# Late loads, first messages and the order of the head in a graph-convolution kernel

## The chip, the core and the metric

One core of a Trainium2 chip runs the whole program in one launch. The metric is the device time of one execution in microseconds (us); the value for a version is the median of its runs. The core has five instruction streams: PE (TensorE, matrix products), DVE (VectorE), ACT (ScalarE), POOL (GpSimd) and SP (SyncE, used here for DMA issues alone). DMAs are issued by SP, ACT or POOL and carried by 16 DMA engines that all of them share.

## What is computed

The reference is one layer of a graph network over 12500 nodes with 128 features and 400000 edges, which are sorted by `dst`:

```python
h   = maximum(layernorm(x), 0) @ W_in2f.T
Wij = (smu(edge_attr @ W_f1.T + b_f1) @ W_f2.T + b_f2) * edge_weight[:, None]
agg = segment_sum(h[dst] * Wij, src)
out = x + smu(agg @ W_o1.T + b_o1) @ W_o2.T + b_o2
```

In the kernel `dst` is thus the node that an edge reads from (its row of h), and `src` the node that its message is added to.

## The kernel before, in words

The 400000 edges are 3125 tiles of 128. Four tiles are a group (`GRP`), eight a super-group (`SUP`). For each group the kernel makes the filter of its 512 edges, fetches their rows of h, multiplies the two, and sends the products, called messages, to buckets in DRAM (`buf`), one bucket for each block of 128 target nodes. A message is one tile of 128 rows of 129 floats; one indirect DMA on POOL (L572) scatters it, so there are 3125 of these. The edges are cut into nine epochs with a set of buckets each. While the messages of epoch k are sent, the buckets of epoch k-1 are read back and added up by matmuls with one-hot matrices (L617) into `agg`. After the last epoch comes the sum of its buckets and the output layers, with no messages left to send.

Within the main block the order of the instructions of PE, DVE, ACT and SP is the order in which the code writes them (`manual_schedule`); POOL's is left to the scheduler. Each engine works through its stream in order, and waits where an operand is not there yet.

A group g passes through small functions: `bins` (DVE) and `count` (PE) find how many earlier edges went to each bucket; `read` (ACT, four activations with an accumulated result) and `number` (DVE) turn that into row indices; `hide` (PE), `bend` (ACT, Gelu), `smooth` (DVE) and `weigh` (PE) make the filter; `pick` (DVE), `gather` (PE) and `take` (ACT) fetch rows of h from a window of 128 rows; `mix` (DVE) multiplies; `turn` (PE) transposes the product; `send` scales it by the edge weights (ACT, L569), casts the row numbers within the target block (DVE, L566) and issues four messages (POOL, L572). The loop runs these for different groups in one round: `turn(g)` and `send(g)` at its start, then the later parts of g+1, the earlier parts of g+2, `bins(g+3)`. Tiles of `ms` have six buffers, tiles of `ix` eight, `pu`, `pc`, `ph`, `pw` and `pt` in PSUM one each. Between these, `step()` takes pieces of other work (the rest of h, L701 to L719), and SP issues the clearing of the first epoch's buckets (L742 to L746).

`load(s)` prefetches for super-group s: `f` (edge attributes, from the fourth on), `rbc` (the edges' rows relative to the window, read back from `rel_dram` and spread over all partitions) and `hw` (the window, read from `h_dram`). In the loop it runs three super-groups ahead.

Ahead of the loop stands the head, written out by hand:

- L345 to L357: loads of the first 512 columns of indices, the first four blocks of x (`HEAD`), weights, the first weights of edges, and one clearing, issued on SP and ACT.
- L358 to L367: the late loads, ten DMAs issued on ACT: the other 94 blocks of x (three parts of 31 blocks, and the last block of 84 rows), the other columns of `w_sb`, two weights and three biases. A part of x is 31 x 128 rows of 512 bytes.
- L644 to L652: the first chunk of `dst` is made relative to its windows, transposed on PE (L308), copied by ACT (L314) and written to `rel_dram` by SP (L315).
- L653 to L659: statistics of four blocks, their deviations (`deviations`: ACT Sqrt, L184, then a reciprocal on DVE), and their rows of h: normalise, transpose, Relu, product with `w_in`, and a split into three bfloat16 parts (L189 to L215), written to `h_dram` by SP (L214).
- L660: `load` for three super-groups.
- L662 to L683: the first groups' functions, up to `mix(0)` (L677), `smooth(1)`, `bins(1)`, `count(1)`, `read(1)`, `pick(1)`, `bins(2)`. `turn(0)` and `send(0)` come at the loop's start.

Activation functions of ACT live in tables; where another table is needed, an ACT_TABLE_LOAD stands in its stream.

Of the kernel before, what the change touches and what calls it, by code (L numbers as in the profile page):

```python
# [9 lines left out]
F32 = mybir.dt.float32  # L10
# [3 lines left out]
AF = mybir.ActivationFunctionType  # L14
# [5 lines left out]
P = 128  # L20
# [19 lines left out]
def gnn_kernel(  # L40
# [19 lines left out]
    nc = tc.nc  # L60
    N, D = x.shape
    R, E = f_t.shape
    NT = E // P
    assert D == P and E % P == 0
    NB = (N + P - 1) // P
    LASTB = N - (NB - 1) * P
    def chunks(total, step):
        return [(a, min(step, total - a)) for a in range(0, total, step)]

    def bin_rows(t, b, n):  # L70
        return t[b * P:(b + n) * P, :].rearrange("(b p) f -> p b f", p=P)
# [4 lines left out]
    for n in PARTS:  # L76
        n = min(n, left)
# [17 lines left out]
    const = ctx.enter_context(tc.tile_pool(name="const", bufs=1))  # L95
# [10 lines left out]
    eps = const.tile([P, 1], F32, name="eps")  # L106
# [20 lines left out]
    CH = 4 * P  # L127
# [9 lines left out]
    w_sb = const.tile([P, NT], F32, name="w_sb")  # L137
# [7 lines left out]
    b2row = const.tile([1, P], F32, name="b2row")  # L145
    b1 = const.tile([P, 1], F32, name="b1")
    bz = const.tile([P, 1], F32, name="bz")
    w_o1 = const.tile([P, P], F32, name="w_o1")
    w_o2 = const.tile([P, P], F32, name="w_o2")
    bo2 = const.tile([P, P], F32, name="bo2")  # L150
# [5 lines left out]
    def clear(k, c, engine):  # L156

        b, n = cleans[c]
        if b == NB - 1:
            m = CAP[k] * ROW // ZP  # L160
            rows = bufs[k][b * CAP[k]:(b + 1) * CAP[k], :].rearrange("(p s) r -> p (s r)", p=ZP)
            for o, w in chunks(m, zero.shape[1]):
                engine.dma_start(rows[:, o:o + w], zero[:, :w])
            return None
        m = (CAP[k] - ZMIN[k]) * ROW // ZP
        rows = bufs[k][b * CAP[k]:(b + n) * CAP[k], :].rearrange("(b c) r -> b c r", c=CAP[k])[:, ZMIN[k]:, :]
        return engine.dma_start(rows.rearrange("b (p s) r -> p b (s r)", p=ZP),
                                zero[:, :n * m].rearrange("p (b m) -> p b m", b=n))
# [3 lines left out]
    HEAD = 4  # L172
    BY = 44
    x_sb = agg.rearrange("p (b d) -> p b d", d=D)
# [73 lines left out]
    with tc.tile_pool(name="ld", bufs=4) as ld, \  # L248
# [106 lines left out]
            fill(i)  # L355
        nc.vector.memset(zero, 0.0)
        clear(0, len(cleans) - 1, nc.scalar)  # L357
        nc.vector.memset(x_sb[:, NB - 1, :], 0.0)  # L358
        for a, n in chunks(NB - 1 - HEAD, 31):
            nc.scalar.dma_start(x_sb[:, HEAD + a:HEAD + a + n, :], bin_rows(x, HEAD + a, n))  # L360
        nc.scalar.dma_start(x_sb[:LASTB, NB - 1, :], x[(NB - 1) * P:N, :])
        nc.scalar.dma_start(w_sb[:, CH:NT], w_col[:, CH:NT])
        nc.scalar.dma_start(w_o1, w_o1_t)
        nc.scalar.dma_start(w_o2, w_o2_t)
        nc.scalar.dma_start(b1, b_o1.rearrange("o p -> p o"))
        nc.scalar.dma_start(b2row, b_f2)
        nc.scalar.dma_start(bo2, b_o2.to_broadcast([P, P]))  # L367

        groups = [(t0 + a, g) for t0, nt in sups for a, g in chunks(nt, GRP)]
        NG = len(groups)  # L370
# [3 lines left out]
        loaded, onehot, bins_of, slots, hidden, taken = {}, {}, {}, {}, {}, {}  # L374

        def load(s):
            if s >= NS:
                return
            t0, nt = sups[s]
            e0, n = t0 * P, nt * P  # L380
            fb = fbufs[s % NF]
            if s > 2:
                nc.sync.dma_start(fb[0:R, :n], f_t[:, e0:e0 + n])
            rb = ld.tile([P, SUP * P], BF, name="rbc")
            nc.sync.dma_start(rb[:, :n], rel_dram[:, e0:e0 + n].to_broadcast([P, n]))
            hw = ld.tile([P, 3 * D], BF, name="hw")
            at = nc.sync.value_load(base_i[0:1, s:s + 1], min_val=0, max_val=N)
            nc.sync.dma_start(hw, h_dram[bass.ds(at, WIN), :])
            loaded[s] = (fb, rb, hw)

        def pick(s):

# [107 lines left out]
        def smooth(g):  # L500
            if g >= NG:
                return
            n = groups[g][1] * P
            sm = edge.tile([P, GRP * P], F32, name="sm")
            nc.vector.scalar_tensor_tensor(sm[:, :n], units_of.pop(g)[:, :n], LIN, hidden[g][:, :n],  # L505
                                           op0=ALU.mult, op1=ALU.add)
            hidden[g] = sm
# [36 lines left out]
        def mix(g):  # L544
            if g >= NG:
                return
            n = groups[g][1] * P
            mt = edge.tile([P, GRP * P], F32, name="mt")
            nc.vector.scalar_tensor_tensor(mt[:, :n], pws.pop(g)[:, :n], b2, rows_of.pop(g)[:, :n],  # L549
                                           op0=ALU.add, op1=ALU.mult)  # L550
            mixed[g] = mt

        def turn(g):

            n = groups[g][1]
            pt = ps1.tile([P, GRP, P], F32, name="pt")
            mt = mixed.pop(g)
            for j in range(n):
                nc.tensor.transpose(pt[:, j, :], mt[:, j * P:(j + 1) * P], ident)  # L559
            mixed[g] = pt  # L560

        def send(g):

            t, n = groups[g]
            ms = msg.tile([P, GRP, ROW], F32, name="ms")
            nc.vector.tensor_copy(ms[:, :n, P], lo_b[:, t:t + n])  # L566
            pt = mixed.pop(g)
            for j in range(n):
                nc.scalar.activation(ms[:, j, 0:P], pt[:, j], AF.Copy, scale=w_sb[:, t + j:t + j + 1])  # L569
            k, ix = epoch[g // PER], taken.pop(g)  # L570
            for j in range(n):
                i = nc.gpsimd.indirect_dma_start(  # L572
                    out=bufs[k][:, :], out_offset=bass.IndirectOffsetOnAxis(ap=ix[:, j:j + 1], axis=0),
                    in_=ms[:, j, :], in_offset=None)

                apart(i, f"slots{k}", f"slots{k}")
                if g < BY:
                    apart(i, "cleared", "filled")

        def apart(i, others, own):  # L580
            tc.declare_no_dep(i.ins, group=others, reason="slots are disjoint")
            tc.add_to_no_dep_group(own, i.ins)
# [67 lines left out]
        one["lowered"]()  # L650
        one["turned"]()
        one["written"]()  # L652
        nc.vector.tensor_scalar(w_f2, w_f2, GC, None, op0=ALU.mult)  # L653
        for b in range(HEAD):
            stats(edge, b)
# [2 lines left out]
        for step in rows_of_h(0, HEAD, *[rw[:, j * GRP:(j + 1) * GRP, 0:P] for j in range(3)], hs, bank):  # L658
            step()  # L659
        for s in range(3):  # L660
            load(s)
        one["binned"]()  # L662
        bins(0)
        hide(0)
# [10 lines left out]
        number(0)  # L675
        take(0)
        mix(0)  # L677
        smooth(1)
        bins(1)
        count(1)  # L680
# [52 lines left out]
        for g in range(NG):  # L733
            s = g // PER
            k = epoch[s]
            g0, ng = eps_of[k][0] * PER, min(eps_of[k][1] * PER, NG - eps_of[k][0] * PER)
            i = g - g0
            if g % PER == 0:
                load(s + 3)
            if i == 0:  # L740
                cleared = 0
            if g < BY:  # L742

                while at_first < min(len(cleans) - 1, -(-(g + 1) * (len(cleans) - 1) // (BY - 6))):
                    apart(clear(0, at_first, nc.sync), "filled", "cleared")
                    at_first += 1  # L746
            elif k + 1 < EPOCHS:
                past = BY if k == 0 else 0
                upto = min(len(cleans), -(-(i + 1 - past) * len(cleans) // (ng - 4 - past)))
                while cleared < upto:  # L750
                    clear(k + 1, cleared, nc.sync)
                    cleared += 1
            if k and i == 0:
                work = [(b, q) for b in range(NB) for q in range(Q[k - 1])]
                done = 0
            if k and i == 1:
                begin(k - 1)
            if k and i == WAIT - 2:
                choose(k - 1, 0)
            lo = hi = 0  # L760
            if k and i >= WAIT:
                lo = len(work) * (i - WAIT) // (ng - WAIT)
                hi = len(work) * (i + 1 - WAIT) // (ng - WAIT)
            turn(g)
            send(g)
            step()
            number(g + 1)
            weigh(g + 1)
            gather(g + 1)
            take(g + 1)  # L770
            parts(k - 1, lo + (hi - lo) // 2)
            mix(g + 1)
            step()
            hide(g + 2)
            bend(g + 2)
            count(g + 2)
            read(g + 2)
            smooth(g + 2)
            if g % PER == 0:
                pick((g + 4) // PER)  # L780
            bins(g + 3)
            parts(k - 1, hi)
            step()
            assert k == 0 or taken_steps == COUNT and next(h_steps, None) is None
# [51 lines left out]
    with tc.If(flag > 0):  # L836
        with tc.tile_pool(name="gl", bufs=1) as gl, tc.tile_pool(name="gps", bufs=1, space=PSUM) as gps:
# [9 lines left out]
            fb = gl.tile([R + 1, P], F32, name="gfb")  # L847
# [116 lines left out]
```

## Time and profile before

| | us |
|---|---|
| median of three runs | 4244.77 |
| lowest, highest | 4242.52, 4252.45 |
| the profiled execution, whole | 4248.45 |
| its span in the trace | 4246.6 |
| PE busy | 3736.8 (88%) |
| DVE busy | 3220.9 (76%) |
| POOL busy | 3017.8 (71%) |
| ACT busy | 2830.2 (67%) |

The span runs from the first to the last instruction of the profiled execution. "Busy" leaves out register, branch and semaphore instructions and the issuing of DMAs by SP and ACT; the indirect DMAs of POOL are counted[...]. In the views, `ACTq` and `SPq` rows are the DMA issues of ACT and SP, and their length is the issue, not the transfer. Matmuls are pipelined, so a high share of PE is not PE at its peak. The granted clock of TensorE was 0.97 of full speed on average over the span.

### The profile page before, as it was taken

To read this page: it belongs to the slowest core of one execution; us is meant where nothing else is said; L and a number is where in the kernel's file an instruction comes from. 1 tells how busy PE (TensorE), PEld (TensorE's weight loads), DVE (VectorE), ACT (ScalarE), POOL (GpSimd) and SP (SyncE) were. 2 spreads that over 40 slices of the span, in tenths; PEclk is the share of its full clock that TensorE was granted. 3 is DMA by queue.
4 is the path that set the end of the run, shared out by engine and by line. 5 is a ranking of instruction groups with operands and counts; after the bars stand their busy time and mean duration, and the time that the engine had idled before them with its cause. 6 is when DMAs were issued, how large, how long until landed. Compare 5 with 4: busy or idle time off the path is not lost. (4 is left out here: it accounts for less than half of the span.)

```text
span 4246.6 us, 74532 instructions
## 1 busy us (share of the span) xinstructions
PE 3736.8 (88%) x18497; PEld 2320.1 (55%) x18794; DVE 3220.9 (76%) x8578; ACT 2830.2 (67%) x11057; POOL 3017.8 (71%) x3133
## 2 busy tenths in 40 slices
PE   5877788999988999979998979998999799898976
PEld 2334434655555655546555546665666566565755
DVE  5886777877767877768877768887888688787865
ACT  4777777776666767657766757776777576676621
POOL 3777777777777777777777777777777777777620
PEclk9999999999999999989999989999999999999988
DMA  7855665766647666756666657775899699786754
GB/s 216 227 148 162 180 173 179 210 205 193 200 145 217 206 197 204 199 156 202 213 196 199 179 176 205 215 214 167 231 231 235 188 246 233 209 233 177 206 165 122
DMA packets 512380, 834.71 MB, mean 197 GB/s; under 512 B 84576, under 2 KB 323398, under 8 KB 511810
## 3 DMA queue, kind: packets, MB, share of 16 engines
q1 hardware_dynamic: 380986, 601.70, 51.8%
q0 software_dynamic: 100000, 206.60, 15.8%
q10 hardware_dynamic: 30952, 21.54, 1.8%
q8 instruction: 152, 2.49, 0.3%
q14 instruction: 290, 2.38, 0.2%
HBM read 456.16 MB, written 373.36 MB: 195 GB/s over the span
## 5 line engine op out<-in xcount | busy, mean ns | idle before, releaser
L572 POOL DMA_INDIRECT buf<-ms,ix x3125 | 3016.8, 965 | 1051.5 <-issue 249.2
L617 PEld LDWEIGHTS pg<-se,rw 128*128 128x128 f32 x8036 | 1096.5, 193 | 158.6 <-issue 21.2
L569 ACT ACTIVATE ms<-pt,w_sb 128x128 f32<-128x128 f32 x3125 | 905.1, 391 | 342.3 <-DMA buf<-ms,ix 163.6
L617 PE MATMUL pg<-se,rw 128*128 128x128 f32 x8036 | 1118.7, 276 | 10.4 <-DVE se L604 10.4
L467 ACT ACTIVATE jk<-pc,nbig 128x98 f32<-128x98 f32 x3125 | 1027.7, 351 | 6.1 <-PE pc L438 5.4
L539 PE MATMUL pw<-sm,w_f 128*128 128x512 f32 x1564 | 883.5, 647 | 40.6 <-DVE sm L505 35.4
L549 DVE SCALAR_TENSOR_TENSOR mt<-pw,b,hg 128x512 f32<-128x512 f32 x782 | 582.8, 745 | 348.2 <-ACT hg L528 345.9
L497 ACT ACTIVATE ge<-pu 128x512 f32<-128x512 f32 x782 | 468.4, 599 | 558.8 <-PE pu L489 537.0
L489 PE MATMUL pu<-f,w_f 128*128 128x512 f32 x1564 | 812.3, 601 | 4.2 <-DVE sm L505 4.1
L559 PE MATMUL pt<-ident,mt 128*128 128x128 f32 x3125 | 495.3, 281 | 298.8 <-DVE mt L549 295.8
L604 DVE TENSOR_TENSOR se<-irow_ps,rw 128x1536 f32<-128x1536 f32 (+1 forms) x345 | 587.5, 1703 | 145.8 <-DMA rw<-buf 125.2
L505 DVE SCALAR_TENSOR_TENSOR sm<-pu,ge 128x512 f32<-128x512 f32 x782 | 535.0, 684 | 209.7 <-ACT ge L497 200.8
L467 ACT ACTIVATION_READ_ACCUMULATOR jk<-pc,nbig 128x1 f32 x3125 | 674.5, 216 | 0.0
L528 ACT ACTIVATE hg<-ph 128x512 f32<-128x512 f32 x782 | 469.1, 600 | 305.3 <-PE ph L520 303.8
L520 PE MATMUL ph<-oh,hw 128*128 128x512 bf16 (+1 forms) x2049 | 631.8, 387 | 16.1 <-issue 0.4
L559 PEld LDWEIGHTS pt<-ident,mt 128*128 128x128 f32 x3125 | 352.9, 142 | 389.7 <-DVE mt L549 382.5
L424 DVE TENSOR_TENSOR co<-co,po 128x98 f16<-128x98 f16 x2353 | 502.6, 214 | 81.1
L520 PEld LDWEIGHTS <-hw 128*128 128x128 bf16 x2346 | 232.9, 99 | 553.6 <-issue 453.7
L410 DVE TENSOR_TENSOR po<-irow_ps,hi_b 128x392 f16<-128x392 f32 x782 | 433.1, 554 | 0.0
L539 PEld LDWEIGHTS pw<-sm,w_f 128*128 128x128 f32 x1564 | 236.8, 191 | 169.7 <-DVE sm L505 164.7
L489 PEld LDWEIGHTS pu<-f,w_f 128*128 128x128 f32 x1564 | 253.6, 196 | 27.9 <-DVE sm L505 5.6
L437 PE MATMUL pc<-co,ones_h 128*128 128x392 f16 x782 | 258.3, 330 | 3.5 <-DVE co L424 3.5
(104 smaller groups left out, 1702.0 us busy)
## 6 DMA issues: line engine op xcount, KB each, us to landing
rw<-buf SPq DMA_DIRECT2D x292, 774.0 KB
rbc<-rel_dram SPq DMA_DIRECT2D x390, 256.0 KB
buf<-zero SPq DMA_DIRECT2D x243, 387.0 KB
buf<-ms,ix POOLq DMA_INDIRECT x3125
buf<-zero SPq DMA_DIRECT2D x193, 258.0 KB
hw<-h_dram SPq DMA_DIRECT2D x391, 96.0 KB
rw<-buf SPq DMA_DIRECT2D x49, 645.0 KB
f<-in_f_t SPq DMA_DIRECT2D x390, 80.0 KB
```

The lines of the kernel that those rows point to most:

```text
L424: nc.vector.tensor_add(co[:, j], co[:, j - 1], po[:, j - 1])
L467: nc.scalar.activation(jk, pc[:, j], AF.Relu, bias=nbig, accum_out=sl[:, j:j + 1])
L489: nc.tensor.matmul(pu[:, :n], w_f1, loaded[g // PER][0][:, o:o + n], start=True, stop=True)
L505: nc.vector.scalar_tensor_tensor(sm[:, :n], units_of.pop(g)[:, :n], LIN, hidden[g][:, :n], op0=ALU.mult, op1=ALU.add)
L520: nc.tensor.matmul(ph[:, :n], hw[:, q * D:(q + 1) * D], oh[:, o:o + n], start=(q == 0), stop=(q == 2))
L539: nc.tensor.matmul(pw[:, :n], w_f2, hidden.pop(g)[:, :n], start=True, stop=True)
L549: nc.vector.scalar_tensor_tensor(mt[:, :n], pws.pop(g)[:, :n], b2, rows_of.pop(g)[:, :n], op0=ALU.add, op1=ALU.mult)
L559: nc.tensor.transpose(pt[:, j, :], mt[:, j * P:(j + 1) * P], ident)
L569: nc.scalar.activation(ms[:, j, 0:P], pt[:, j], AF.Copy, scale=w_sb[:, t + j:t + j + 1])
L572: i = nc.gpsimd.indirect_dma_start(out=bufs[k][:, :], out_offset=bass.IndirectOffsetOnAxis(ap=ix[:, j:j + 1], axis=0), in_=ms[:, j, :], in ...
L604: nc.vector.tensor_tensor(se[:, :m], irow_ps.unsqueeze(1).to_broadcast([P, m, P]), rows_in[c][:, :m, P:P + 1].to_broadcast([P, m, P]), op= ...
L617: nc.tensor.matmul(pgs[0][:, g, :], rows_in[c][:, o, 0:P], sel[c][:, o, :], start=(q == 0), stop=(q == Q[k] - 1))
```

## The change

The late loads become a function, `late_loads()`, that is called behind the first rows of h; their issuing engine becomes GpSimd. Ahead of each part of x and of the columns of `w_sb`, one column of the destination is set to zero by VectorE, so that these loads wait for that instruction. In the place where the late loads stood, one dummy activation with Sqrt is run. `load(s)` loses its last part, the window of h, which becomes `window(s)`; the first three `load`s come ahead of the first statistics, the three `window`s stay behind the writing of h. `turn(0)` and `send(0)` move from the loop to the place right behind `mix(0)`.

```diff
@@ in place of L358 to L367
-        nc.vector.memset(x_sb[:, NB - 1, :], 0.0)
-        for a, n in chunks(NB - 1 - HEAD, 31):
-            nc.scalar.dma_start(x_sb[:, HEAD + a:HEAD + a + n, :], bin_rows(x, HEAD + a, n))
-        nc.scalar.dma_start(x_sb[:LASTB, NB - 1, :], x[(NB - 1) * P:N, :])
-        nc.scalar.dma_start(w_sb[:, CH:NT], w_col[:, CH:NT])
-        nc.scalar.dma_start(w_o1, w_o1_t)
-        nc.scalar.dma_start(w_o2, w_o2_t)
-        nc.scalar.dma_start(b1, b_o1.rearrange("o p -> p o"))
-        nc.scalar.dma_start(b2row, b_f2)
-        nc.scalar.dma_start(bo2, b_o2.to_broadcast([P, P]))
+        spare = const.tile([P, 1], F32, name="spare")
+        nc.scalar.activation(spare, eps, AF.Sqrt)
+
+        def late_loads():
+
+            nc.vector.memset(x_sb[:, NB - 1, :], 0.0)
+            parts_of_x = chunks(NB - 1 - HEAD, 31)
+            for a, n in parts_of_x:
+                nc.vector.memset(x_sb[:, HEAD + a, 0:1], 0.0)
+            for a, n in parts_of_x:
+                nc.gpsimd.dma_start(x_sb[:, HEAD + a:HEAD + a + n, :], bin_rows(x, HEAD + a, n))
+            nc.gpsimd.dma_start(x_sb[:LASTB, NB - 1, :], x[(NB - 1) * P:N, :])
+            nc.vector.memset(w_sb[:, CH:CH + 1], 0.0)
+            nc.gpsimd.dma_start(w_sb[:, CH:NT], w_col[:, CH:NT])
+            nc.gpsimd.dma_start(w_o1, w_o1_t)
+            nc.gpsimd.dma_start(w_o2, w_o2_t)
+            nc.gpsimd.dma_start(b1, b_o1.rearrange("o p -> p o"))
+            nc.gpsimd.dma_start(b2row, b_f2)
+            nc.gpsimd.dma_start(bo2, b_o2.to_broadcast([P, P]))
@@ load(s)
-            hw = ld.tile([P, 3 * D], BF, name="hw")
-            at = nc.sync.value_load(base_i[0:1, s:s + 1], min_val=0, max_val=N)
-            nc.sync.dma_start(hw, h_dram[bass.ds(at, WIN), :])
-            loaded[s] = (fb, rb, hw)
+            loaded[s] = (fb, rb)
+            if s > 2:
+                window(s)
+
+        def window(s):
+
+            hw = ld.tile([P, 3 * D], BF, name="hw")
+            at = nc.sync.value_load(base_i[0:1, s:s + 1], min_val=0, max_val=N)
+            nc.sync.dma_start(hw, h_dram[bass.ds(at, WIN), :])
+            loaded[s] += (hw,)
@@ the head
         one["written"]()
+        for s in range(3):
+            load(s)
         nc.vector.tensor_scalar(w_f2, w_f2, GC, None, op0=ALU.mult)
...
             step()
         for s in range(3):
-            load(s)
+            window(s)
+        late_loads()
         one["binned"]()
...
         mix(0)
+        turn(0)
+        send(0)
         smooth(1)
@@ the loop
-            turn(g)
-            send(g)
+            if g:
+                turn(g)
+                send(g)
             step()
```

## The prediction

> **What bounds the kernel now.** I read the groups of instructions first, to find the engine that sets the pace. Columns: line, engine, operation, output<-inputs, count | busy us, mean ns | idle us just before it, and what ended most of that.
> ```profile
> L572 POOL DMA_INDIRECT buf<-ms,ix x3125 | 3016.8, 965 | 1051.5 <-issue 249.2
> ```
> GpSimd (POOL) scatters 3125 messages at 0.965 us each; the timeline below shows 0.30 us of issue between neighbours, so 1.27 us a message at best. Then the stretches (length, busy us and count by engine, granted clock, DMA share, GB/s):
> ```profile
> 8.00:36.00 28.00, 3.00 (x6) 1.05 (x6) 2.78 (x14) 4.06 (x6) 0.00 (x0) 1.00 1.01 293
> 59.00:110.00 51.00, 43.66 (x153) 19.69 (x155) 41.82 (x140) 38.73 (x154) 37.05 (x39) 0.96 0.88 224
> 1200.00:1800.00 600.00, 543.59 (x2669) 334.52 (x2707) 452.01 (x1200) 416.77 (x1652) 454.79 (x472) 0.97 0.66 194
> ```
> From 1200 to 1800 there are 472 messages in 600 us, 1.27 us each: exactly POOL's pace, with PE close behind (544 of 600 us). The first message starts at 58.58 and the last ends at 4069.85; 3125 x 1.27 = 3969, so stalls of POOL after its start are only 4011 - 3969 = 42 us. Behind the last message stand 177 us of final sums, which the change leaves alone. So the time is start of the first message + 3969 + 42 + 177, and a change at the head counts nearly in full. What sets the start is in the timeline (start us, length us, engine, line, operation; ACTq and SPq are DMA issues):
> ```profile
> 7.43 0.34 ACTq L163 DMA_DIRECT2D buf<-zero  x1
> ...
> 9.29 6.69 ACTq L360 DMA_DIRECT2D agg<-in_x  x1
> ...
> 16.44 6.33 ACTq L360 DMA_DIRECT2D agg<-in_x  x1
> 22.86 6.89 ACTq L361 DMA_DIRECT2D agg<-in_x  x1
> ...
> 32.68 1.28 ACT L314 ACT_TABLE_LOAD   x1 [16.27 <-DMA agg<-in_x]
> 33.98 0.60 ACT L314 ACTIVATE oh<-pg 128x512 bf16<-128x512 f32 x1
> 34.59 1.28 ACT L184 ACT_TABLE_LOAD   x1
> ...
> 35.88 0.30 ACT L184 ACTIVATE rstd<-mv,eps 128x4 f32<-128x4 f32 x1
> ...
> 43.61 0.41 SPq L214 DMA_DIRECT2D h_dram<-hs  x1
> ...
> 58.58 1.11 POOL L572 DMA_INDIRECT buf<-ms,ix  x1 [57.01 <-ACT ms L569]
> 59.99 0.96 POOL L572 DMA_INDIRECT buf<-ms,ix  x1 [0.30 <-issue]
> ...
> 64.68 0.96 POOL L572 DMA_INDIRECT buf<-ms,ix  x1 [1.20 <-ACT hg L528]
> ```
> ScalarE's queue sits in late loads from 8.0 to 32.65 us, because the transfers fill the 16 DMA engines (share 1.01, 293 GB/s) and the issue waits for room. L314's input, the transposes of L308, had ended at 11.87, L184's (the last statistics) at 12.37. The whole front of the kernel waits in that queue.
>
> **The change, part by part.**
>
> *Late loads off ScalarE.* Ten DMA issues leave. The root's table is asked for by a dummy activation at 7.8, ready near 9.3, while ScalarE would only wait. L314 then starts at 11.9 and ends at 12.5; L184 follows at 12.53 instead of 35.88: **-23.35 us**. That contains one table load of 1.28 (two stood behind the queue, one is left, under cover). Copy needs none of its own: L208 and L212 run as Copy behind L184 with no load between. From rstd to the writing of h is a chain of arithmetic (35.88 to 43.61, 7.7 us), so h goes out near 20.3.
>
> *Targets read back ahead of h.* SP's rbc loads wait for rel_dram's write (then issued near 12.5), which lands long before 20.3, so h is not held back on SP. Behind h, three window loads follow each other without rbc loads between. Taken at nothing: before, hw0 was issued at 46.41 and used at 50.80 with PE busy in between, and the 0.87 us that VectorE waited for rbc is not on PE's chain. If the write were late, h and everything after it would wait on SP; there are some 5 us of cover.
>
> *The memsets.* One 128x128 memset (0.17) moves behind h's last part and four of one column (0.06 each, by eps's row) are new on VectorE, ahead of binned, bins(0) and smooth(0), for which PE waits: 0.17 + 4 x 0.06 = **+0.4 us**. They also hold the x and w_sb loads back until 20.7.
>
> *First messages early.* Before, mix(0) ends at 53.72, but turn(0) stood behind count(1), which waits for bins(1) and began at 55.78; transposes 56.31, ms activations 57.90, message 58.58. Moved, transposes run from 53.75, the activations from about 54.6, the message at about 55.3: **-3.3 us** for message 1. But group 1's first message (64.68) hangs on its own chain, relieved only of turn(0)'s 1.06 us on PE and some of ScalarE: **-0.9 us**. POOL sends four messages in 5.1 us and waits again. What lasts is group 1's shift: -23.35 + 0.4 - 0.9 = **-23.8**, and for message 1 it is -26.2, a start at 32.4.
>
> *Late loads on POOL.* The disputed cost: no plain DMA on POOL is in this trace. POOL is idle from 20.7 to 32.4, so 11.7 us are covered; beyond that each us delays message 1, and all that follow. Each x part has 31 x 128 = 3968 rows of 512 bytes. Ends: if an instruction costs what an indirect one does whatever its rows, ten cost at most 10 x 1.27 = 12.7 us, five of which have no memset to wait for and can go in the idle head: nothing on the path. If the 0.965 us of 128 rows is all per row (7.5 ns), a part costs 29.9 us and three 89.7. In between stands the nearest row for the same transfers: 6.3 to 6.9 us of issue each, when the queue waits for the engines to drain it; the ten took 24.6 us on ScalarE. By that row POOL is held until 20.7 + 24.6 = 45.3 and message 1 starts near 45.6: -13 us.
> The Trainium skill speaks to this. DMA: Bandwidth & Descriptors, section Anatomy of one DMA — SWDGE (gpsimd) path, says descriptor generation is small and variable, and "You can emit a lot of descriptors before the incremental cost shows up". By the rule the sum is -23.8, by the drain row -13, by the indirect row spread over its rows about +50. I take the rule's end: the 965 ns include reading 128 indices, which a plain copy doesn't do, and ScalarE's 6.7 us are 2.03 MB at 303 GB/s, so they are a rate of draining, not of generating, and count only if POOL's queue too is short. Against the change, SBUF — State Buffer (section SBUF: two separate sides) says GpSimd can't write descriptors while VectorE holds the shared port. The row weighs against that here: messages kept 965 ns on average, 0.96 when undisturbed, beside a VectorE busy 76%. I add nothing.
>
> *What the loads then collide with.* 7.6 MB move from an empty stretch (8 to 36) into 21 to about 60, beside h's windows, the clearing of buf and the first messages, which also stand behind them in POOL's own queue. The loop's start used 0.88 of the DMA engines at 224 GB/s, so about 254 at full share. Some 2 MB drain before the clears begin near 28; the other 5.5 MB at 254 are 22 us of DMA work, against spare room of 0.12 x 51 = 6 us in the first 51 us. The rest must push clears and prefetches back. Prefetches run a super-group ahead (two groups, 10 us), and ms has six buffers, 30 us of messages, ahead of the landing they wait for. Lower bound 0, upper 22 - 6 = 16; I take **+6**, what is left of the excess once the 10 us of prefetch absorb it.
>
> Sum: -23.8 + 6 = **-17.8**. The profiled execution took 4248.45 us, 1.85 of it outside its span of 4246.6; it would become 4230.7. Its distance to the median of 4244.77 is noise of single runs, so I subtract from the median: **4227**.
>
> **The rivals.**
> *POOL is held at the drain rate* (chance 0.22). For it: the ACT rows of 6.3 to 6.9; against it: they show ScalarE's queue only. Message 1 near 45.6, while groups 1 to 6 are ready behind it, so group 1's 1.2 us gap closes: -13 to -14, and contention mostly hides in it: about 4231, between 4228 and 4240.
> *POOL pays per row* (0.25; the slower side). Mechanism: descriptor generation for the three x parts at 2.4 to 7.5 ns a row, in front of message 1. It decides from (58.6 - 20.7 - 9 for the small ones)/3 = 9.6 us a part, 2.4 ns a row. At 7.5 ns: 20.7 + 89.7 + 9 = 119.4 instead of 58.6, +61, less up to 15 of the early stalls that ready groups fill: 4290; midway 4262. For it: the only POOL row, 965 ns for 128 rows; against it: the index reading in that row.
> *The DMA engines give the gain back* (0.08). The work until 210 us is conserved, and the loop's share is already 0.9 (228 GB/s from 110 to 210); if prefetches starve until the backlog is gone, the 16 us of the upper bound and a stall on ms's landing remain: 4238 to 4246. An order of the loads that lets them run in the head before h (POOL's order is not written out by hand) would belong here.
>
> **How the numbers follow.** The main case (0.45) gives 4219 to 4236: the giveback between 0 and 16 against -23.8. 0.3% is 12.7 us, about what a measurement of this kernel can tell from no change; faster is below 4232. Main case 0.36 of its 0.45 below that, drain 0.13 of 0.22, giveback none: 0.49 faster. Slower (above 4257.5): per row, 0.19 of its 0.25. Same: the rest, 0.32. The range leaves out 0.05 below 4217 and about 0.13 above 4272.
>
> **What would show it.** L314 should start near 12, L214's issue near 20, with no long ACTq rows ahead. POOL's own rows of direct DMA tell the cases apart: about 1 us each (main case), 6 to 7 (drain), above 10 (per row, slower). Message 1 should be near 32, group 1 near 41. Stretches after 1200 should keep 472 messages in 600 us. If POOL's idle time before 250 us exceeds before's 107 - 57 = 50 us, contention took the rest. The prediction is wrong if message 1 starts after 45, or if the last message has moved less than the first ones.

## The result, and the profile after

The changed kernel took 4231.73 us (median of nine runs, 4228.93 to 4237.49), the kernel before 4246.68 in its nine runs: ratio 0.9963, 95% interval 0.9953 to 0.9974. The forecast was 4227 from 4244.77, a ratio of 0.9958; the change is 15.0 us where 17.8 were forecast. In per cent it is 0.37, with an interval of 0.26 to 0.47, so it lies about at the 0.3% from which the prediction counted a kernel as faster. The profiled execution has a span of 4228.5 us.

The head went as the prediction had it. The timeline of the changed kernel:

```profile
7.81 1.28 ACT L359 ACT_TABLE_LOAD   x1 [7.81 <-DMA b<-in_b_f]
...
11.78 0.60 ACT L314 ACTIVATE oh<-pg 128x512 bf16<-128x512 f32 x1 [2.48 <-PE pg L308]
...
12.28 0.30 ACT L184 ACTIVATE rstd<-mv,eps 128x4 f32<-128x4 f32 x1
...
20.01 0.39 SPq L214 DMA_DIRECT2D h_dram<-hs  x1
```

L184 starts at 12.28 instead of 35.88, the writing of h at 20.01 instead of 43.61. What had no row before is GpSimd's own part, the timeline of that engine alone (the last bracket is the idle time before the row, and who ended it):

```profile
1.56 0.73 POOL L372 DMA_DIRECT2D w_o<-in_w_o_t  x1
...
20.43 0.66 POOL L369 DMA_DIRECT2D agg<-in_x  x1 [15.95 <-DVE w_sb L370]
21.06 5.24 POOL L368 DMA_DIRECT2D agg<-in_x  x3
26.29 0.77 POOL L371 DMA_DIRECT2D w_sb<-in_w_col  x1
32.55 1.09 POOL L587 DMA_INDIRECT buf<-ms,ix  x1 [5.49 <-ACT ms L584]
...
40.07 0.96 POOL L587 DMA_INDIRECT buf<-ms,ix  x1 [2.57 <-ACT hg L543]
42.73 0.96 POOL L587 DMA_INDIRECT buf<-ms,ix  x1 [1.70 <-ACT ms L584]
50.07 0.96 POOL L587 DMA_INDIRECT buf<-ms,ix  x1 [6.39 <-DMA agg<-in_x]
53.88 0.98 POOL L587 DMA_INDIRECT buf<-ms,ix  x1 [2.85 <-DMA w_sb<-in_w_col]
57.88 0.96 POOL L587 DMA_INDIRECT buf<-ms,ix  x1 [3.02 <-DVE ix L491]
```

A part of x, 3968 rows, holds GpSimd for 5.24 / 3 = 1.75 us. Message 1 starts at 32.55, 26.0 us earlier. But messages 5 to 9 then come in jerks, and two of the waits end in a late load's landing. By message 13 only 10.5 us of the 26.0 are left: 15.5 us are given back. From there the two kernels run nearly alike for some hundred messages (the lead is 11.6 at message 240). The stretch of the stall and the stretch of 600 us (columns as in the prediction):

```profile
36.00:59.00 23.00, 9.23 (x25) 3.52 (x25) 7.43 (x29) 6.44 (x27) 6.01 (x7) 0.68 1.04 352
...
1200.00:1800.00 600.00, 545.70 (x2683) 336.19 (x2722) 454.23 (x1205) 417.47 (x1655) 455.77 (x474) 0.97 0.65 195
```

From 36 to 59 all engines are idle most of the time, PE busy 9.23 of 23 us, while the DMA engines are full (busy share 1.04, 352 GB/s). Later the pace is 474 messages in 600 us, 472 before. Who waited for whom from 38 to 60 us (total, times, longest):

```profile
ACT hg L543 <- PE ph L535: 17.0, 2, 16.7
...
DVE base_i L292 <- DMA rw<-in_dst_col: 13.2, 1, 13.2
PE pg L299 <- DVE base_f L293: 13.0, 1, 13.0
POOL buf L587 <- DMA agg<-in_x: 6.4, 1, 6.4
```

Two waits stand side by side. GpSimd waits for late loads. And VectorE stands 13.2 us at L292 for the next chunk of `dst`. PE waits for VectorE, and ACT for PE. SyncE's issue of that fetch in the changed kernel; then the issue and VectorE's wait before:

```profile
41.35 0.36 SPq L288 DMA_DIRECT2D rw<-in_dst_col  x1
```
```profile
61.99 0.36 SPq L288 DMA_DIRECT2D rw<-in_dst_col  x1
...
66.69 0.21 DVE L292 COPY base_i<-rw 1x64 int32<-1x64 int32 x1 [1.33 <-DMA rw<-in_dst_col]
```

From issue to VectorE's instruction the fetch takes 12.6 us (to 53.98) in the changed kernel, 4.7 us before.

### The profile page after: what moved, and what is told of

Its sections match the earlier page's. It is cut to its first block, busy times and chain, and to the rows that moved or that the text cites. A ratio compares the mean times of both kernels' runs of the same rounds, so it can differ in the third digit from the quotient of the medians.

```text
span 4228.5 us, 74544 instructions
## 1 busy us (share of the span) xinstructions
PE 3733.3 (88%) x18497; PEld 2317.0 (55%) x18794; DVE 3223.7 (76%) x8582; ACT 2823.5 (67%) x11054; POOL 3022.2 (71%) x3143
```

## The experiments

The theories. **A**: a message on GpSimd's queue can't go until the DMA issued eight places before it on that queue has landed. Behind the late loads that makes messages 4 to 8 wait for the last block, the three parts of x and w_sb in turn, and 9 on for messages that are themselves behind the loads in the queue. **B**: the bytes crowd the DMA engines, and SyncE's prefetches and clears come late; that is the prediction's own account. **D**, found in the profile of one experiment (e4), is the piece of B that can be pointed at: the fetch for L292. **P**, drawn from the trace of e7 and not set up before it: in the loop GpSimd is the pace, so a DMA issued there costs its own row.

The first four ran on another chip, which granted TensorE 0.90 of its clock and on which the kernel before took 5304 us. GpSimd is not the pace there: e1 sends 372 messages from 1200 to 1800 us, where the changed kernel sends 474. Their whole times say nothing on this change, and only their first 75 us are used.

| start of message (us) | 1 | 5 | 7 | 8 | 9 | 13 | lead at 13 |
|---|---|---|---|---|---|---|---|
| before | 58.58 | 64.68 | 67.21 | 68.59 | 70.60 | 76.35 | 0 |
| changed | 32.55 | 40.07 | 50.07 | 53.88 | 57.88 | 65.82 | 10.5 |
| first part only in the head (e1) | 32.85 | 42.05 | 44.68 | 45.95 | 47.21 | 52.63 | 23.7 |
| clears from group 10 (e2) | 32.91 | 42.55 | 50.61 | 55.02 | 56.29 | 63.81 | 12.5 |
| 24 parts (e3) | 46.93 | 52.08 | 54.60 | 57.05 | 58.31 | 63.36 | 13.0 |
| late loads on SyncE (e4) | 31.63 | 41.00 | 43.53 | 44.80 | 65.52 | 72.62 | 3.7 |
| changed, again (e5) | 32.88 | 42.38 | 49.63 | 53.20 | 58.45 | 66.37 | 10.0 |
| fetch early (e6) | 33.60 | 42.88 | 49.92 | 53.95 | 55.21 | 60.26 | 16.1 |
| eight parts over the loop (e7) | 32.14 | 40.92 | 43.55 | 44.81 | 46.08 | 51.35 | 25.0 |
| messages in the loop (e8) | 36.42 | 42.38 | 49.80 | 53.27 | 59.27 | 67.21 | 9.1 |

The starts are read off each timeline's rows of GpSimd, one execution for each run. "Changed" and e5 are the same kernel: two executions of it differ by 2.3 us at message 5 and by 0.5 at message 13.

**e1: only the first part of x in the head.**

```diff
-            for a, n in parts_of_x:
-                nc.gpsimd.dma_start(x_sb[:, HEAD + a:HEAD + a + n, :], bin_rows(x, HEAD + a, n))
+            part_of_x(0)
...
+        later = {12: lambda: part_of_x(1), 24: lambda: part_of_x(2), 40: weights}
...
                 send(g)
+            if g in later:
+                later[g]()
```

> The changed kernel, but only the first part of x and the last block follow the first rows of h; the other two parts of x and the other columns of w_sb go out behind the messages of groups 12, 24 and 40. Theory A (a message on GpSimd waits until the DMA issued eight places before it on that queue has landed, so messages 5 to 12 wait for the late loads): message 5 to 12 no longer stall, the lead at message 13 is 22 to 24 us instead of 10.5, and the whole is some 12 us below the changed kernel, near 4219; each later load holds back the message eight places behind it by less than 2 us. Theory B (the bytes themselves push SyncE's clears and prefetches back): the same bytes still come in the first 210 us at a DMA share of 0.9, so a part of the giveback comes back by group 50: near 4226.

Messages 5 to 13 keep their pace, and the lead at 13 is 23.7. So the giveback belongs to the two later parts of x and to w_sb. The run doesn't tell A from B or D: its trace has no wait at L292 either. On the whole and on what later loads cost it says nothing, because of the chip.

**e2: the clears later.**

```diff
-                while at_first < min(len(cleans) - 1, -(-(g + 1) * (len(cleans) - 1) // (BY - 6))):
+                while at_first < min(len(cleans) - 1, -(-(g + 1 - 10) * (len(cleans) - 1) // (BY - 16))):
```

> The changed kernel, with the clearing of the first epoch's buckets starting at group 10 instead of 0 and ending at the same group. Theory A: the late loads still have to land before messages 5 to 8 can go; without 2.3 MB of clears beside them of the 12.3 MB moved from 20 to 60 us they land some 5 us sooner, so a giveback of about 10 of the 15.5 us stays at message 13. Theory B: SyncE's queue has nothing to be pushed back by, the giveback falls to 0 to 3 us at message 13.

Messages 7 and 8 are as late as in the changed kernel, the lead at 13 is 12.5, so some 13 us of the giveback stay. B in its simple form, clears that push the prefetches back, falls. A had about 10: the loads did not land sooner. The wait at L292 shrinks only from 13.2 to 9.0 us.

**e3: 24 parts of x.**

```diff
-            parts_of_x = chunks(NB - 1 - HEAD, 31)
+            parts_of_x = chunks(NB - 1 - HEAD, 4)
```

> The changed kernel, with the 93 blocks of x loaded by 24 DMAs of 4 blocks (512 rows) instead of 3 of 31, same bytes, same place. Theory A: from the ninth late load on GpSimd each issue waits for the landing of the one eight before, so the idle time moves ahead of the loads' own rows and message 1 starts between 38 and 46 instead of 32.55; message 13 about as late as before or a little earlier. Theory B: no such waits, 24 rows of about 0.6 us end near 36, message 1 near 37, the stalls of messages 5 to 8 stay. The rows also give the price of a row: at the 1.75 us of 3968 rows and 0.57 us of 128 rows, 0.3 ns a row, so some 0.7 us for 512.

GpSimd's timeline:

```profile
20.42 0.70 POOL L369 DMA_DIRECT2D agg<-in_x  x1 [15.95 <-DVE agg L366]
21.11 10.02 POOL L368 DMA_DIRECT2D agg<-in_x  x13
34.25 0.75 POOL L368 DMA_DIRECT2D agg<-in_x  x1 [3.12 <-DVE co L439]
...
46.93 1.03 POOL L587 DMA_INDIRECT buf<-ms,ix  x1 [0.65 <-DVE base_f L293]
```

Thirteen parts go out in a row at 0.77 us each, then the fourteenth waits until 34.25. Eight places before it is the sixth. GpSimd's queue had moved 1.68 MB from 20 to 31 us, and the last block with six parts is 1.62 MB; that the sixth part was whole only near 34 is argued, the view doesn't name it. From there the loads go out one or two at a time, with waits between. Message 1 goes at 46.93, where B had 37 and A 38 to 46: A, and a little beyond its end. A limit on rows or bytes instead of on DMAs doesn't fit both kernels: here GpSimd stops behind 13 parts (6656 rows, 3.4 MB), in the changed kernel three parts and w_sb (11904 rows of x, 7.4 MB in all) go out without a stop.

**e4: the late loads on SyncE.**

```diff
-                nc.gpsimd.dma_start(x_sb[:, HEAD + a:HEAD + a + n, :], bin_rows(x, HEAD + a, n))
+                nc.sync.dma_start(x_sb[:, HEAD + a:HEAD + a + n, :], bin_rows(x, HEAD + a, n))
```

... (and the other late loads in the same way)

> The changed kernel, with the late loads issued by SyncE at the same place in its order (behind the three windows) instead of GpSimd. Theory A: messages 5 to 12 keep their pace, since nothing that is on GpSimd's queue is slow; the stall moves to where the first prefetch that stands behind the loads on SyncE is needed (super-group 3, group 6, messages 25 and on), 10 us or more there. Theory B: messages 5 to 8 stall about as in the changed kernel, as the same bytes move at the same time.

Messages 5 to 8 keep their pace beside the same loads (DMA share 1.01, 307 GB/s from 36 to 59 us): A. The stall then comes at message 9, not at 25 as I had written. SyncE's rows, and the waits from 40 to 70 us:

```profile
25.45 13.87 SPq L368 DMA_DIRECT2D agg<-in_x  x3
39.37 7.11 SPq L369 DMA_DIRECT2D agg<-in_x  x1
...
56.95 0.71 SPq L288 DMA_DIRECT2D rw<-in_dst_col  x1
```
```profile
DVE base_i L292 <- DMA rw<-in_dst_col: 19.9, 1, 19.9
```

The first thing to be missed behind the loads on SyncE is not the prefetch of a super-group but the fetch of the second chunk of `dst`. VectorE waits for it in order, 19.9 us. That sent me back to the 13.2 us at L292 in the changed kernel, and to theory D.

The other four ran on a chip like the first (before: 4244.41, 18 runs).

**e5: the changed kernel again.**

> The changed kernel itself, as the measure for the others of this job. Both theories: message 1 near 32.5, lead over before of 26 at message 1 and 10 to 11 at message 13, the whole 0.996 of before where TensorE is granted nearly its full clock.

4232.65 us (4225.90 to 4236.69, six runs), ratio 0.9967 [0.9955, 0.9979]; lead 25.7 at message 1, 10.0 at 13.

**e6: the fetch early.**

```diff
         for s in range(3):
             load(s)
+        nxt = head_of(1)
+        nxt["fetched"]()
...
-                it = head_of(c)
+                it = head_of(c) if c > 1 else nxt
...
-                    yield it[name]
+                    yield (lambda: None) if c == 1 and name == "fetched" else it[name]
```

> The changed kernel, with the fetch of the second chunk of indices (dst and src, 512 KB) issued on SyncE behind the three first read-backs instead of in the loop. In the changed kernel VectorE waits 13.2 us for it at L292 and the other engines behind VectorE. Theory D (that late fetch is what costs, GpSimd's own waits lie under it): no wait at L292, the giveback at message 13 falls from 15.5 to 0 to 3 us. Theory A (eight DMAs in flight on GpSimd's queue): the wait at L292 goes as well, but messages 7 and 8 stay at 50 and 54, and the lead at message 13 gains only the 2 to 5 us by which L292 came later: 13 to 15.

The first rows are VectorE's L292 for the second and the third chunk. Then come ACT's scaling of messages 5 to 8 and GpSimd's messages 5 to 9:

```profile
43.49 0.33 DVE L292 COPY base_i<-rw 1x64 int32<-1x64 int32 x1
...
81.45 0.31 DVE L292 COPY base_i<-rw 1x64 int32<-1x64 int32 x1 [6.50 <-DMA rw<-in_dst_col]
```
```profile
40.77 1.16 ACT L584 ACTIVATE ms<-pt,w_sb 128x128 f32<-128x128 f32 x4
```
```profile
42.88 0.96 POOL L587 DMA_INDIRECT buf<-ms,ix  x1 [4.45 <-ACT hg L543]
44.14 1.07 POOL L587 DMA_INDIRECT buf<-ms,ix  x1 [0.30 <-ACT jk L482]
49.92 0.96 POOL L587 DMA_INDIRECT buf<-ms,ix  x1 [4.71 <-ACT jk L482]
53.95 0.96 POOL L587 DMA_INDIRECT buf<-ms,ix  x1 [3.07 <-ACT jk L482]
55.21 0.95 POOL L587 DMA_INDIRECT buf<-ms,ix  x1 [0.30 <-DVE ms L581]
```

The wait at L292 for the second chunk is gone and the engines work on (PE busy 20.7 of the 23 us from 36 to 59, 9.2 in the changed kernel), but messages 7 and 8 stand at 49.92 and 53.95, as late as in the changed kernel. From message 9 on there is no gap. So D alone is out and A stands; the lead at 13 is 16.1. The view names ACT for the waits of messages 7 and 8, but it names the last event that it saw: ACT had scaled all four messages of the group by 41.93, and message 6, of the same group, went at 44.14. In the changed kernel, e2, e5 and e8 the view names a part of x for message 7 and w_sb for message 8. For the third chunk VectorE then waits 6.50 us, and it costs no message: the lead is 15.8 at message 29 and 16.0 at message 33. The whole, 4227.57 us (four runs, ratio 0.9958 [0.9943, 0.9973]), lies below the changed kernel's, with overlapping intervals.

**e7: eight parts over the loop.**

```diff
+        def part_of_x(i):
+            a, n = chunks(NB - 1 - HEAD, 12)[i]
...
...
+        later = {5 * i: (lambda i=i: part_of_x(i)) for i in range(1, 8)}
+        later.update({40 + 5 * i: (lambda i=i: weights(i)) for i in range(3)})
```

> The changed kernel, with x's late blocks in eight parts of at most 12 (768 KB): the first behind the first rows of h, one more behind the messages of every fifth group, then w_sb in three parts. Theories A and D agree: neither wait is left, the lead is 23 to 24 at message 13 and stays within 2 us of that up to message 128; the whole near 0.9945 of before, some 12 us below the changed kernel. Theory B (the bytes cost wherever they go in the loop's start): the lead at message 128 is back to 15 or less.

Up to message 13 as expected, with a lead of 25.0. But it melts: 19.5 at message 64, 14.4 at 128, 10.0 at 240. By the sign set before the run (15 or less at message 128) that is B's outcome, and A with D had it wrong. GpSimd's timeline around the second part:

```profile
65.33 1.02 POOL L594 DMA_INDIRECT buf<-ms,ix  x1 [0.30 <-ACT jk L489]
66.35 1.08 POOL L375 DMA_DIRECT2D agg<-in_x  x1
67.74 0.99 POOL L594 DMA_INDIRECT buf<-ms,ix  x1 [0.30 <-DMA buf<-ms,ix]
...
75.44 0.97 POOL L594 DMA_INDIRECT buf<-ms,ix  x1 [0.30 <-ACT ms L591]
78.14 0.96 POOL L594 DMA_INDIRECT buf<-ms,ix  x1 [1.74 <-ACT ge L519]
```

A load in the loop costs its own row, 1.05 to 1.08 us for a part of x and 0.58 for a third of w_sb: 7 x 1.07 + 3 x 0.58 = 9.2 us of the 15.0 lost from message 13 to 240. And the message eight places behind this load (78.14; the seventh is the row ahead of it) waits another 1.4 us over the usual 0.30; the same is seen behind the loads at 94.64 and 178.06, not behind all. Rows and these three waits are 13.7 of the 15.0 us, so P and A carry most of it by this reading, which came after the run. B would forecast the same melting, and the run that divides them, the same loads issued by SyncE in the loop, was not tried. VectorE also waits 4.5 us at L292 again, at 104 us, where neither wait was to be left. Nor does the melting last: the lead is 14.5 at message 400 and 20.7 at the last one, and what wins it back is open. The whole, 4237.95 us (eleven runs, ratio 0.9981 [0.9972, 0.9990]), is no better than the changed kernel; the profiled execution, 4227.73, was the fastest of the eleven, and why the median lies 10 us above it stays open.

**e8: group 0 sent in the loop again.**

```diff
         mix(0)
-        turn(0)
-        send(0)
...
-            if g:
-                turn(g)
-                send(g)
+            turn(g)
+            send(g)
```

> The changed kernel, with the transposes and messages of group 0 back at the loop's start. Theory A: message 1 near 35.9, but messages 5 on wait for the late loads' landing all the same, so the lead at message 13 and the whole are those of the changed kernel within 1 us: sending early buys nothing. The prediction's working: 0.9 us lost from message 5 on.

Message 1 is 3.5 us later than in the run of the changed kernel beside it, message 5 starts at the same 42.38, the lead at 13 is 9.1 against 10.0, the whole 4231.04 against 4232.65. Sending early buys four messages, and nothing that the runs can show behind them; the 0.9 us at message 13 can't be told from the 0.5 between two executions of one kernel.

## Why the prediction was right, and where not

- *Late loads off ScalarE, -23.35.* Right: L184 moved by 23.6 us, h by 23.6.
- *Read-backs ahead of h, nothing.* Right: h was not held back. PE now waits 0.76 us for the first window (it didn't before), which the sum didn't have.
- *Memsets, +0.4.* Too high: they overlap at VectorE's ends of instructions, and `binned` starts 0.09 us behind h's last part.
- *First messages.* Message 1 at 32.55, forecast 32.4; message 5 at 40.07, forecast near 41. That message 1's shift would not last was right. The -0.9 that this edit was to give group 1 did not show: e8, without the edit, has message 5 at the same 42.38 as e5.
- *GpSimd's price.* The choice of the rule, many rows at little cost, over both rows was right: 1.75 us for 3968 rows, 0.56 for 128, so (1.75 - 0.56)/3840 = 0.31 ns a row. The slower rival needed 2.4. The rival of the drain rate needed 6 to 7 us a part and is out as well.
- *The giveback, +6.* The term that was mis-sized. From message 1 to message 13 the kernel gives back 15.5 us; counted as the sum counts it, from group 1's -23.8, it is 13.3, toward the upper bound of 16 that I gave and turned down. I took the DMA engines' bytes, with prefetch and the six buffers of `ms` as cover. The runs show two waits in its place. One is GpSimd's eight DMAs in flight. With D removed (e6) the lead at 13 is 16.1, with neither wait (e7) 25.0. That makes A 8.9 us at most: e7 also moves fewer bytes there, and 1.4 of the 8.9 stand at message 1 already. The other is the fetch of the second chunk, which has no prefetch: e6 against the changed kernel, 16.1 - 10.0 to 10.5, makes D 5.6 to 6.1 us beside A. The second could be read off the text before: in `others()` the fetch is followed by its use with hardly a step between. The first could not: the 107.9 us in 348 pieces that the profile before puts down to landings of GpSimd's own messages are 0.31 us each, the gap that stands between any two messages.
- *The signs.* GpSimd's idle time ahead of its messages up to 250 us, less the wait for message 1, is 67 us against 50 before; this sign said that time was given back, but it can't tell full DMA engines from a limit on GpSimd's queue. And one sign of being wrong came true: the last message moved less (18.2 us) than the first (26.0). It was badly set, since the sum itself has -26.2 for message 1 and -17.8 for the whole.

The whole came to 15.0 us, more than the 10.5 at message 13. The last message led by 18.2 us in the first profiled execution and by 11.4 in the second, both against the same one of before. Runs of one kernel spread by 8 us and more, so what the stretch behind message 13 adds can't be told from that spread here. With nothing won behind message 13 the forecast of -17.8 would have been off by 7.3 us; its closeness is in part luck.

The best version seen, e6, is the changed kernel with the fetch moved; its gain over it, 5 us in medians, is inside the intervals. Late loads issued on GpSimd in the empty stretch from 10 to 20 us, which might avoid both waits, were not tried.

## What to carry to other kernels

When a queue is moved to an idle engine, ask not only how long the issue holds that engine but how many of its DMAs may be under way before the next must wait: big slow transfers ahead of small urgent ones on one queue hold the urgent ones up although the engine is idle. When transfers fill the DMA engines, look for the fetch that stands next to its use: here VectorE waited 13.2 us for it, and no wait for a prefetch of the loop stands in that stretch. Even so such a wait costs only what the pacing engine loses by it: 5.6 us or more at the second chunk, nothing at the third. And an edit that brings one item forward earns nothing where the items behind it wait for something else.

## What the runs showed of the hardware that was not expected

Plain DMAs on GpSimd cost hardly more for many rows: 0.55 to 0.73 us at 128 rows, 0.77 at 512, 1.07 at 1536, 1.75 at 3968, against 0.96 for an indirect one of 128. The eighth DMA behind a large one waits for its landing: in the changed kernel messages 7 and 8 for a part of x and for w_sb, and by the same count in e3 among the loads, in e6 and e7 among messages. Whether this number belongs to the queue or to the program's semaphores was not told apart. And the kernel before took 5304 us on a chip that granted TensorE 0.90 of its clock where it took 4244 on another at 0.97: 25% more time with 7% less clock. PE is not busier there (470 of 600 us in e1 from 1200 to 1800, 546 in the changed kernel on the first chip), so the clock alone doesn't explain it, and the cause stays open.
